# The decay of a running sum, read from PSUM instead of SBUF

## The chip, the cores and the metric

The kernel runs on one core of one Trainium2 chip. The metric is the device time of one execution in microseconds; beside the median of the runs there is one profiled execution, whose rows give every duration used here. The core has a tensor engine (PE, with its weight loads, PEld), a vector engine (DVE), a scalar engine (ACT), GpSimd (POOL) and SyncE (SP), which issues transfers. Each engine takes its instructions in the order in which they stand in its own queue; between engines, semaphores order the work. Data lives in SBUF; PE writes its results to PSUM, from where DVE and ACT read them. POOL and the transfers do not touch PSUM.

## The reference, cut to what matters

Four layers follow one another, each adding to x what it computes from the normalised x: an attention with 49 agents, a two-way running sum (RWKV), a shift with a small convolution, and a long convolution by FFT. x is (32, 192, 56, 56) in float32. Only the second layer is touched:

```python
def step(carry, kv_t):
    p, q, o = carry
    kt, vt = kv_t
    no = jnp.maximum(o, u + kt)
    A = jnp.exp(o - no)
    Bw = jnp.exp(u + kt - no)
    y = (A * p + Bw * vt) / (A * q + Bw)
    ...
    return ((A2 * p + B2 * vt, A2 * q + B2, no2), y)
...
k = jnp.einsum('btc,dc->btd', xs, Wk)
v = jnp.einsum('btc,dc->btd', xs, Wv)
r = jnp.einsum('btc,dc->btd', xs, Wr)
real_w = -jnp.exp(w_decay)
x_fwd = wkv_scan(real_w, u, k, v)
x_bwd = jnp.flip(wkv_scan(real_w, u, jnp.flip(k, 1), jnp.flip(v, 1)), 1)
x_bi = 0.5 * (x_fwd + x_bwd)
h = jax.nn.sigmoid(r) * x_bi
...
out = jnp.einsum('btc,dc->btd', h, Wo)
```

Between the gate and the last product h is normalised over the channels. Without the maxima that keep the exponentials in range, each step is p = d * p + exp(k) * v and q = d * q + exp(k), with one decay d = exp(-exp(w_decay)) for each channel. That is what the kernel's scans compute, over the 3136 pixels of an image, forwards and backwards.

## The kernel before

The layers run one after another on the core: the filter and the attention, then `scan_pairs`, then the channel blocks. A check at the end of `scan_pairs` decides whether a slower guarded form is run in its place; here it isn't.

`scan_pairs` works on images in pairs. The 192 channels of two images make 384 rows, so three tiles of 128: two hold 128 channels of one image each, the third the remaining 64 channels of both. The 3136 pixels are cut into four pieces of 784 (`MC`), so a tile of work is 128x784. There are 16 pairs of images and four pieces, so 64 iterations.

In an iteration, `forwards` for one piece of the next pair and `backwards` for one piece of the present pair run interleaved, with `finish` for the piece before:

- `normed` loads three tiles of x (SP) and normalises them (ACT, L1054).
- `forwards`: PE makes keys and values; ACT takes exp of the keys out of PSUM (L1103), DVE multiplies the values in PSUM by them (L1108). `scan` then makes two running sums for each tile, one over exp(k) v and one over exp(k). ACT inverts the second (L1079, L1080) and DVE multiplies (L1118).
- `backwards`: PE makes the gate r; ACT reads it out of PSUM (L1132) and turns it into a sigmoid (L1136, L1137); `scan` runs in the other direction; then the inverse and three steps on DVE (L1140 to L1142).
- `finish`: PE takes the channel mean away (`centre`), ACT squares out of PSUM (L1157), PE averages the squares (`mean_w`), ACT takes the logarithm out of PSUM (L1166) and the root (L1167); PE multiplies by Wo, DVE scales the product in PSUM (L1180) and adds x (L1183), ACT squares the sum (L1190).

`scan` (L1057 to L1076) issues for each of the two sums: a POOL copy of the carried value into the edge column (L1067), the scan on DVE (L1072), a POOL copy of the last column into the carry (L1073), and one DVE step that adds the present pixel with its bonus (L1074). The scan's operation is out[i] = decay * out[i-1] + data[i]. Its decay is one column of `decay`, a 128x2 tile in SBUF, spread over 784 elements by a stride of zero (column 0 for the first two tiles, column 1 for the third: `of`). An iteration has 12 scans, the stage 768.

PSUM is used up by one pool of four tiles, each 128 x 2 x 512 float32, so two banks of 512. `turned` gives the next of them. A product of 784 pixels fills 392 columns (`HM`) of each bank; columns 392 to 511 of every bank are free. Products for two tiles are written by `_Pairs.outer` (lines 834 and 837), for one tile by `_Pairs.inner` (lines 844 and 847). 17 tiles are taken in an iteration.

The order in the engines' queues is not the order of the text. A scheduler places every instruction, and decides each wait from what the instructions read and write.

Of the kernel before, what the change touches and what calls it, by code (L numbers as in the profile page):

```python
# [7 lines left out]

# [2 lines left out]

# [7 lines left out]
F32 = mybir.dt.float32  # L21
I32 = mybir.dt.int32
AF = mybir.ActivationFunctionType
ALU = mybir.AluOpType
AX = mybir.AxisListType
PSUM = bass.MemoryType.PSUM
# [10 lines left out]
MC = 784  # L37
NM = N // MC
HM = MC // 2
# [26 lines left out]
BANK = 512  # L66
# [784 lines left out]
def scan_pairs(ctx: ExitStack, tc: tile.TileContext, a, k, x1, st_a, st_c, x2, rs2, count):  # L851
# [5 lines left out]
    nc = tc.nc  # L857
# [2 lines left out]
    kp = ctx.enter_context(tc.tile_pool(name="s_k", bufs=3 * NM))  # L860
    wp = ctx.enter_context(tc.tile_pool(name="s_w", bufs=9))
    sp = ctx.enter_context(tc.tile_pool(name="s_s", bufs=2))
    pp = ctx.enter_context(tc.tile_pool(name="s_p", bufs=4, space=PSUM))
    pairs = _Pairs(nc)

    def small(name, shape):
        return cp.tile(shape, F32, name=name, tag=name)

    def turned():
        ps = pp.tile([128, 2, BANK], F32, name="ps", tag="ps")  # L870
        return ps, ps[:, :, :HM], [ps[:, h, :HM] for h in range(2)]

    def parts(t):
# [20 lines left out]
    rows = ((0, 128), (1, 64))  # L894
    cb = small("cb", [128, 2])
    ps, _, _ = turned()
    for out, cols in ((ps[:, 0, 0:1], slice(0, 128)), (ps[0:64, 0, 1:2], slice(128, C)), (ps[64:128, 0, 1:2], slice(128, C))):
        for i, n in rows:
# [20 lines left out]
    decay, near, far = small("decay", [128, 2]), small("near", [128, 2]), small("far", [128, 2])  # L919
# [13 lines left out]
    nc.vector.tensor_tensor(near, near, z, ALU.mult)  # L933
    nc.vector.tensor_tensor(decay, near, far, ALU.add)

    eps = small("eps", [128, 1])
    nc.vector.memset(eps, 4.0 * LN_EPS)
    kept_a, kept_c = small("kept_a", [128, 2, NB // 4, 2]), small("kept_c", [128, 2, NB // 4])
# [5 lines left out]
    def of(t):  # L944
        return slice(0, 1) if t < 2 else slice(1, 2)
# [19 lines left out]
    def grouped(src):  # L965

        n = src[0].shape[1]
        ps, _, _ = turned()
        for t, r in enumerate((slice(0, 64), slice(64, 128))):
            nc.tensor.matmul(ps[:, t, :n], group[0], src[t], start=True, stop=False)  # L970
            nc.tensor.matmul(ps[:, t, :n], group[1][r], src[2][r], start=False, stop=True)
        pairs.inner(group, [ps[:, 1, n : 2 * n]], [[s] for s in src])
        return ps[:, :, :n], ps[:, 1, n : 2 * n]
# [83 lines left out]
    def scan(s, m, t, carry, rev):  # L1057

        b, e = s.bv[m][t], s.ek[m][t]
        c = eu[:, of(t)]  # L1060
        got = []
        for i, src in enumerate((b, e)):
            z = wp.tile([128, MC + 1], F32, name="pq"[i], tag="pq", bufs=5)
            edge, last = (MC, 0) if rev else (0, MC)
            out, before = (z[:, 0:MC], z[:, 1:]) if rev else (z[:, 1:], z[:, 0:MC])
            at = carry[t][i]
            nc.gpsimd.tensor_copy(z[:, edge : edge + 1], at)  # L1067
            if rev:
                out, data = out[:, ::-1], src[:, ::-1]
            else:  # L1070
                data = src[:, :]
            nc.vector.tensor_tensor_scan(out, decay[:, of(t)].to_broadcast([128, MC]), data, at, ALU.mult, ALU.add)  # L1072
            nc.gpsimd.tensor_copy(at, z[:, last : last + 1])  # L1073
            nc.vector.scalar_tensor_tensor(before, src, c, before, ALU.mult, ALU.add)  # L1074
            got.append(before)
        return got  # L1076
# [12 lines left out]
    def forwards(s, m, behind=()):  # L1089
        s.ek[m] = [kp.tile([128, MC], F32, name="ek", tag="ek", bufs=3 * NM + 1) for _ in range(3)]  # L1090
        s.bv[m] = [kp.tile([128, MC], F32, name="bv", tag="bv") for _ in range(3)]
        s.y[m] = [kp.tile([128, MC], F32, name="y", tag="y", bufs=3 * NM + 4) for _ in range(3)]
        xn = normed(s, m)
        for tiles in ((0, 1), (2,)):
            for wt in (wk, wv):
                ps = [turned() for _ in tiles]
                if len(tiles) == 2:
                    pairs.outer(wt, [q[2] for q in ps], xn)
                else:
                    pairs.inner(wt, ps[0][2], xn)  # L1100
                for t, (_, both, _) in zip(tiles, ps):
                    if wt is wk:
                        nc.scalar.activation(  # L1103
                            s.ek[m][t].rearrange("p (h n) -> p h n", h=2), both, AF.Exp,
                            accum_out=s.seen[:, 0, 3 * m + t : 3 * m + t + 1],
                        )
                    else:
                        nc.vector.tensor_tensor(  # L1108
                            s.bv[m][t].rearrange("p (h n) -> p h n", h=2), both,
                            s.ek[m][t].rearrange("p (h n) -> p h n", h=2), ALU.mult,  # L1110
                        )
                if wt is wk and tiles == (0, 1):
                    for later in behind:
                        later()
            for t in tiles:
                num, den = scan(s, m, t, s.fore, False)
                inverse(s, den, m, t, 1)
                nc.vector.tensor_tensor(s.y[m][t], num, den, ALU.mult)  # L1118

    def backwards(s, m):  # L1120

        xn = normed(s, m)
        h = s.y[m]
        for tiles in ((0, 1), (2,)):
            ps = [turned() for _ in tiles]
            if len(tiles) == 2:
                pairs.outer(wr, [q[2] for q in ps], xn)
            else:
                pairs.inner(wr, ps[0][2], xn)
            for t, (_, both, _) in zip(tiles, ps):  # L1130
                g = wp.tile([128, MC], F32, name="g", tag="t")
                nc.scalar.activation(  # L1132
                    g.rearrange("p (h n) -> p h n", h=2), both, AF.Exp, scale=-1.0,
                    accum_out=s.seen[:, 3, 3 * m + t : 3 * m + t + 1],
                )
                nc.scalar.activation(g, g, AF.Ln, bias=1.0)  # L1136
                nc.scalar.activation(g, g, AF.Exp, scale=-1.0)  # L1137
                num, den = scan(s, m, t, s.back, True)
                inverse(s, den, m, t, 2)
                nc.vector.tensor_tensor(num, num, den, ALU.mult)  # L1140
                nc.vector.tensor_tensor(h[t], h[t], num, ALU.add)
                nc.vector.tensor_tensor(h[t], h[t], g, ALU.mult)  # L1142
            yield
# [121 lines left out]
    ps, _, _ = turned()  # L1265
# [502 lines left out]
@with_exitstack  # L1768
def all_blocks(ctx: ExitStack, tc: tile.TileContext, a, k, out):
    nc = tc.nc  # L1770
    NB = out.shape[0]
    dp = ctx.enter_context(tc.tile_pool(name="dram", bufs=1, space=DRAM))

    def scratch(name, shape):
        return dp.tile(shape, F32, name=name, tag=name)

    x1, x2 = scratch("x1", [NB, C, N]), scratch("x2", [C, 2, S + 1, NB // 2, S])
    filt, rs2 = scratch("filt", [C, KS * KS]), scratch("rs2", [C, 2, NB // 4, 2])
    spectra = scratch("spectra", [84, C, 2, 42])
    st_a, st_c = scratch("st_a", [128, 2, NB // 2, 9]), scratch("st_c", [2, 64, 2, NB // 2, 9])  # L1780
    with tc.tile_pool(name="a_r", bufs=1) as rp, tc.tile_pool(name="a_x", bufs=2) as xp:
        ready = _Ready(rp, xp)
        make_filter(tc, a, k, filt, spectra, lambda: ready.load(nc, a, k))
        attention(tc, a, ready, x1, st_a, st_c)
    with tc.tile_pool(name="count", bufs=1) as cp:
        count = cp.tile([1, 1], I32, name="count", tag="count")
        scan_pairs(tc, a, k, x1, st_a, st_c, x2, rs2, count)
        n = nc.values_load(count[0:1, 0:1], min_val=0, max_val=128)
        with tc.If(n > 0):
            scan_guarded(tc, a, k, x1, x2, rs2)  # L1790
    channel_blocks(tc, a, k, x2, rs2, spectra, out)
# [104 lines left out]
```

## Time and profile before

| What | Value |
|---|---|
| Median of 3 runs | 12294.04 us (12291.52 to 12297.86) |
| The profiled execution, its own time | 12294.66 us |
| Its span, first to last instruction | 12292.8 us |
| Granted clock of PE, mean over the span | 0.966 |
| First scan starts; last scan starts | 4919.3 us; 8307.4 us |
| Stage of the scans, 4919 to 8309 | 3390 us |
| Transfers over the span | 59 GB/s |

The span is the time from the first instruction to the last in the profiled execution; its rows add up to this span and not to the median, which comes from other executions. The stage of the scans is about 28% of the span (3390 of 12292.8). A row of the profile names the line, the engine, the operation, the tiles written and read, and their shape; "busy" is the sum of the durations, and durations of neighbouring instructions on one engine overlap a little, so that the time from start to start is shorter than the duration. "Idle before" is time in which the engine had nothing to run, with the instruction that ended it.

### The profile page before, as it was taken

How to read it: one execution, taken by the hardware profiler on the slowest of the kernel's cores; microseconds unless marked ns; L12 is line 12 of the kernel's file. 1: busy time of each engine (PE TensorE's matmuls, PEld its weight loads, DVE VectorE, ACT ScalarE, POOL GpSimd, SP SyncE). 2: the span in 40 equal slices, each digit the busy share in tenths (PEclk: the TensorE clock that was granted, in tenths of full speed). 3: DMA queues.
4: the chain of work that ended last, by engine and by line, in shares of the span. 5: the costliest groups of instructions: out<-in, count | busy, mean ns of one | idle time of the engine just before them, and what ended most of it. 6: DMA issues, size and time to landing. Idle time of an engine off the chain costs nothing. (4 is left out here: it accounts for less than half of the span.)

```text
span 12292.8 us, 164375 instructions
## 1 busy us (share of the span) xinstructions
PE 11329.2 (92%) x62734; PEld 7107.7 (58%) x62734; DVE 10836.4 (88%) x15489; ACT 6205.0 (50%) x11808; POOL 2250.7 (18%) x2228
## 2 busy tenths in 40 slices
PE   7999999999999999788888888888999999999999
PEld 3555555655555555333333333336777777777777
DVE  6888888888888887999999999997888888888888
ACT  3555555555555554566666666663333333333333
POOL 0000000000000000655555555551000000000000
PEclk9999999999999999999999999999999999999999
DMA  2111111111111111244344433442111111111111
GB/s 69 40 42 46 52 41 40 40 40 40 40 40 40 42 50 44 75 103 100 95 97 103 101 94 97 103 101 65 44 41 45 41 44 42 44 42 44 42 43 29
DMA packets 930055, 719.69 MB, mean 59 GB/s; under 512 B 770325, under 2 KB 807236, under 8 KB 920124
## 3 DMA queue, kind: packets, MB, share of 16 engines
q1 hardware_dynamic: 919020, 683.39, 21.7%
q10 hardware_dynamic: 10240, 25.70, 0.8%
q8 instruction: 500, 8.19, 0.3%
q14 instruction: 295, 2.42, 0.1%
HBM read 403.47 MB, written 240.65 MB: 52 GB/s over the span
## 5 line engine op out<-in xcount | busy, mean ns | idle before, releaser
L572 DVE SCALAR_TENSOR_TENSOR o<-v_a,att_w,o 128x896 f32<-128x896 f32 (+1 forms) x1024 | 1053.8, 1029 | 418.6 <-ACT v_a L546 291.5
L1763 ACT COPY y<-ps 64x252 f32<-64x252 f32 (+1 forms) x2376 | 808.2, 340 | 1135.0 <-PE ps L1757 1104.8
L1681 PE MATMUL ps<-fixed,real 84*84 84x112 f32 x6144 | 1090.9, 259 | 0.0
L1681 PE MATMUL ps<-fixed,imag 84*84 84x112 f32 x6144 | 1089.5, 259 | 0.0
L1688 ACT COPY z<-ps 84x448 f32<-84x448 f32 x768 | 405.6, 528 | 1218.5 <-PE ps L1681 1217.0
L1086 POOL MEMSET f<- 128x1 f32 x96 | 8.9, 99 | 4726.3 <-DMA st_c<-st 4721.3
L1681 PEld LDWEIGHTS ps<-fixed,real 84*84 84x84 f32 x6144 | 784.0, 153 | 134.2 <-issue 95.8
L1681 PEld LDWEIGHTS ps<-fixed,imag 84*84 84x84 f32 x6144 | 763.8, 153 | 0.0
L1079 ACT ACTIVATE q<-q 128x784 f32<-128x784 f32 x384 | 328.2, 855 | 802.5 <-DVE q L1074 633.1
L834 PE MATMUL ps<-sq,fixed 128*128 128x392 f32 x512 | 297.3, 743 | 428.6 <-ACT sq L1157 428.6
L572 DVE SCALAR_TENSOR_TENSOR o<-v_c,att_w,o 128x448 f32<-128x448 f32 (+1 forms) x1024 | 635.0, 620 | 5.1
L585 PE MATMUL ps<-xs_a,gk_a 128*98 128x448 f32 (+1 forms) x1536 | 637.1, 495 | 0.0
L589 ACT ACTIVATE pr<-ps,low 98x896 f32<-98x896 f32 (+1 forms) x384 | 352.3, 918 | 559.9 <-DVE low L587 559.9
L586 PE MATMUL ps<-xs_c,gk_c 125*98 125x448 f32 (+1 forms) x1536 | 631.6, 492 | 0.0
L1547 POOL TENSOR_TENSOR mat<-tap,tap 114x114 f32<-114x114 f32 x96 | 40.8, 425 | 3166.1 <-PE ps L1607 2313.2
L677 PE MATMUL ps<-gq_a,xs_a 128*112 128x294 f32 x1792 | 602.8, 417 | 19.2 <-DVE pq L682 19.2
L1698 PE MATMUL ps<-z,fixed 84*114 84x448 f32 x1536 | 608.8, 539 | 0.0
L834 PE MATMUL ps<-x,weights 128*128 128x392 f32 x1536 | 577.4, 519 | 27.5 <-DVE bv L1108 14.2
L678 PE MATMUL ps<-gq_c,xs_c 125*112 125x294 f32 x1792 | 594.5, 412 | 0.0
L1655 PE MATMUL re<-y,fixed 128*84 128x420 f32 (+1 forms) x1152 | 532.3, 543 | 8.7 <-ACT y L1763 7.6
L1655 PE MATMUL im<-y,fixed 128*84 128x420 f32 (+1 forms) x1152 | 526.9, 538 | 0.0
L690 ACT ACTIVATE pq<-pq 112x1176 f32<-112x1176 f32 x224 | 265.3, 1184 | 498.9 <-DVE pq L682 376.0
(367 smaller groups left out, 29245.2 us busy)
## 6 DMA issues: line engine op xcount, KB each, us to landing
x<-x SPq DMA_DIRECT2D x576, 392.0 KB
x<-x SPq DMA_DIRECT2D x512, 196.0 KB
x<-x SPq DMA_DIRECT2D x192, 399.0 KB
out_x<-x SPq DMA_DIRECT2D x384, 196.0 KB
x<-in_x SPq DMA_DIRECT2D x32, 1568.0 KB
x<-x SPq DMA_DIRECT2D x32, 1568.0 KB
x<-in_x SPq DMA_DIRECT2D x64, 392.0 KB
rd<-rd ACTq DMA_DIRECT2D x128, 196.0 KB
```

The source lines that it names most:

```text
L572: nc.vector.scalar_tensor_tensor(dst, tap(i), dww[:, t, i : i + 1], dst, ALU.mult, ALU.add)
L585: mm(ps[P2, h, :n], g[:, cols], xs_a[j][:, px], start=True, stop=False)
L586: mm(ps[P2, h, :n], gk_c[0:KC, 2 * j + h, cols], xs_c[j][0:KC, px], start=False, stop=True)
L589: nc.scalar.activation(pr[:, :, :n], ps[P2, :, :n], AF.Exp, bias=low[:, j, p : p + 1], accum_out=sums[:, j, p : p + 1])
L677: mm(ps[:SUB, i, :HA], xs_a[j][:, px], g, start=True, stop=False)
L678: mm(ps[:SUB, i, :HA], xs_c[j][0:KC, px], gq_c[0:KC, 2 * j + (q + i) // ns], start=False, stop=True)
L834: mm(out, aa, srcs[t][h], start=True, stop=False)
L1655: nc.tensor.matmul(ps[:, : n * 84], f2[:, i, :], y[:, i0 : i0 + n].rearrange("p g s u -> p (g s u)"), start=True, stop=True)
L1681: nc.tensor.matmul(ps[:84, i * 2 * S : (i + 1) * 2 * S], part[:, i0 + i].rearrange("p s u -> p (s u)"), f3[:, m, :], start=(m == 0), stop= ...
L1688: nc.scalar.copy(z[:, i0 : i0 + n].rearrange("p g m w -> p (g m w)"), ps[:84, : n * 2 * S])
L1698: nc.tensor.matmul(got, f4[:, m, :], z[:, i0 : i0 + n, m, :], start=(m == 0), stop=(m == 1))
L1763: nc.scalar.copy(y[64 * m : 64 * m + 64, 2 * g0 + i : 2 * (g0 + n) : 2], got[64 * i : 64 * i + 64, :, :, m, :])
```

## The change

The pool of four tiles becomes four tiles that are made once, each with a name of its own (`ps0` to `ps3`), and `turned` gives them in turn. As they live for the whole stage, something may be kept in them: the two columns of `decay` are copied into columns 392 and 393 of the first bank of the first tile, where no product is written, and the scans read this copy, `pace`, in place of `decay`.

```diff
+import itertools
...
-    pp = ctx.enter_context(tc.tile_pool(name="s_p", bufs=4, space=PSUM))
+    pp = ctx.enter_context(tc.tile_pool(name="s_p", bufs=1, space=PSUM))
     pairs = _Pairs(nc)
+
+    banks = [pp.tile([128, 2, BANK], F32, name=f"ps{i}", tag=f"ps{i}") for i in range(4)]
+    turns = itertools.cycle(banks)
...
     def turned():
-        ps = pp.tile([128, 2, BANK], F32, name="ps", tag="ps")
+        ps = next(turns)
         return ps, ps[:, :, :HM], [ps[:, h, :HM] for h in range(2)]
...
     nc.vector.tensor_tensor(decay, near, far, ALU.add)
 
+
+    pace = banks[0][:, 0, HM : HM + 2]
+    nc.vector.tensor_copy(pace, decay)
     eps = small("eps", [128, 1])
...
-            nc.vector.tensor_tensor_scan(out, decay[:, of(t)].to_broadcast([128, MC]), data, at, ALU.mult, ALU.add)
+            nc.vector.tensor_tensor_scan(out, pace[:, of(t)].to_broadcast([128, MC]), data, at, ALU.mult, ALU.add)
```

Nothing else is edited. The scheduler orders the stage anew with the changed accesses.

## The prediction

> **What bounds the kernel now.** I began with the page's busy times: no engine is full over the whole span, so the stage of the scans has to be read alone. The scans' own line gives its bounds: the first of 768 starts at 4919 us, the last at 8307.4, so the table by windows was asked for 4919 to 8309.
>
> ```profile
> PE 11329.2 (92%) x62734; PEld 7107.7 (58%) x62734; DVE 10836.4 (88%) x15489; ACT 6205.0 (50%) x11808; POOL 2250.7 (18%) x2228
> ```
>
> ```profile
> 4919.00:8309.00 3390.00, 2808.14 (x10237) 1277.79 (x10236) 3296.25 (x3377) 2148.40 (x3691) 1922.99 (x1698) 0.92 0.39 97
> ```
>
> In the stage the columns are PE, PEld, DVE, ACT, POOL. DVE works 3296 of 3390 us (97%) and is idle 94; PE is busy 2808 (83%). Nothing can be gained except by shorter DVE instructions or out of those 94 us. Next the groups of instructions of DVE and POOL in the same window (busy, mean ns, idle before them):
>
> ```profile
> L1072 DVE TENSOR_TENSOR_SCAN p<-decay,b,bv 128x784 f32<-128x784 f32 x192 | 353.6, 1842 | 0.0
> L1074 DVE SCALAR_TENSOR_TENSOR p<-bv,eu,p 128x784 f32<-128x784 f32 x384 | 386.8, 1021 | 0.1
> L1140 DVE TENSOR_TENSOR p<-p,q 128x784 f32<-128x784 f32 x190 | 183.8, 968 | 12.4 <-ACT q L1080 12.1
> L1108 DVE TENSOR_TENSOR bv<-ps,ek 128x784 f32<-128x784 f32 x192 | 180.3, 965 | 4.9 <-PE ps L837 4.9
> L1180 DVE TENSOR_TENSOR sq<-ps,rd 128x784 f32<-128x784 f32 x186 | 178.6, 968 | 60.7 <-PE ps L837 55.7 <-ACT q L1079 1.9 <-ACT g L1136 1.7
> L1073 POOL COPY f<-p 128x1 f32<-128x1 f32 x192 | 338.9, 1765 | 316.9 <-DVE p L1072 309.0
> ```
>
> A scan costs 1.84 us where any other 784-element operation costs 0.96 to 1.02. The idle time is mostly 61 us before the products with Wo (L1180), which wait for PE; a scan waits for ACT only where its keys come late (19 us, 9 of them at the start). POOL copies one column in 1.77 us, yet DVE waits for none of them. Last PE's line of time, around one iteration:
>
> ```profile
> 6500.79 5.60 PE L834 MATMUL ps<-sq,fixed 128*128 128x392 f32 x8 [8.83 <-ACT sq L1157]
> 6506.32 1.89 PE L837 MATMUL ps<-sq,fixed 64*128 64x392 f32 x8
> ...
> 6518.45 2.90 PE L834 MATMUL ps<-x,weights 128*128 128x392 f32 x8
> 6521.28 1.59 PE L837 MATMUL ps<-x,weights 64*128 64x392 f32 x8
> ...
> 6527.15 1.58 PE L844 MATMUL ps<-x,weights 128*128 128x392 f32 x4
> 6528.66 1.54 PE L847 MATMUL ps<-x,weights 128*64 128x392 f32 x8
> ```
>
> A group for two tiles takes 4.35 us (6518.45 to 6522.80), for one tile 2.98 (6527.15 to 6530.13, where the next begins); two records are one matmul. After 8.83 us of waiting the same eight first records take 5.53 us in place of 2.83: PE comes back at a lower clock.
>
> **Part 1: the scan's operand.** 768 scans read their decay from PSUM. No row has a scan with a PSUM operand. From below: the nearest one-pass row, L1074 at 1.02, would give 768 x (1.84 - 1.02) = 630 us back. From above: L1108 and L1180 read PSUM, L1140 reads only SBUF, and they differ by at most 3 ns; even 10 ns would be 8 us. I take zero: L1140 and L1074 have two SBUF operands of four bytes and run one element per step, so that pair is not what makes the scan take two. The trace's scan takes one step more per element than L1074 (0.82 us over 784 elements). [...]
>
> **Part 2: POOL.** The copies before and behind each scan (L1067, L1073) may get shorter, since a scan now has one SBUF operand. DVE waits for no copy, so nothing is gained; ACT's wait for POOL at L1079 is hidden, because DVE waits for ACT's inverses (L1140) only 12 us in the stage. That 12 us is the most this can bring.
>
> **Part 3: the bank.** This is where I see the cost. `pace` lies in columns 392 and 393 of the first bank of tile 0, and a matmul group that writes tile 0 begins in this bank. The instruction order of the changed program with its waits shows the ordering by bank, not by column: 193 matmul groups into tile 0 wait for a scan, and scans wait behind ACT's readers of tile 0 (39 times L1132, 33 L1166, 22 L1157) and 18 times for PE. Before there was neither. 280 uses of tile 0 lie in 193 windows between two scans. In a window DVE may do only what isn't a scan, while PE fills tile 0 and ACT or DVE empties it. Both queues are in order: behind the matmul that waits stand the groups of the other three tiles, and behind the scan that waits stands all of DVE. And as the order bunches four to eight scans (1.76 us apart), PE waits up to ten microseconds and returns slow.
>
> Cost of a window = length of the hand-over less DVE's other work in it. DVE's work by start-to-start times in its line of time: 0.95 for L1074, 0.88 for a two-operand step. The kinds, with their counts in the order:
> - Centre, square, mean, Ln (25 windows): half a two-tile group at the slow clock (half of 5.53, plus 1.52 for its half-row matmuls with no partner beside them) 4.3; ACT's second inverse pass, which stands in front, 0.85; square 0.8; mean group 4.35; two Ln of 0.8: 11.9. DVE has two L1074 and six steps, 7.2. Missing 4.7: 118 us. In 8 more the gate's group follows on tile 0 in place of the Ln: 11.9 - 1.6 + 2.98 + 0.8 = 14.1, missing 6.9: 55 us.
> - Wo after the scans, then the next pair's keys and values (22): rest of the Wo pair 3.0 (half of 2.90, plus 1.59), its third tile 2.98, keys 4.35, values 4.35: 14.7 before the first product L1108, against 9.2 of DVE work: 5.5 each, 121 us.
> - The same with Wo already under way (29): in 22 PE begins 1.2 late, finishing the group of the window before, and has the Wo pair, its third tile, keys and values (16.0) to do against two scans and 10.1 of other work (13.6), 3.6; in 7 only today's 1.3 (55.7 us over the 42 waits of L1180 for PE): 88 us.
> - Third tile's keys (8): slow one-tile group 2.98 x 5.53/2.83 = 5.8, ACT 0.8, against two L1074 and a step, 2.78: 3.8, 30 us.
> - One group and one reader (43): between 0 and (half-group and half-rows 3.0 + 0.8 - 1.83) 2.0; nearer to the upper end, as DVE's step in the window waits for ACT's two inverse passes too: 1.5, 65 us.
> - The other 58: 5.4 to 6.3 us of DVE work over one group and one reader (at most 4.35 + 0.8): nothing. If that cover goes, 58 x 2 = 116 us.
>
> Sum 477 us. It takes the place of today's waits for PE and ACT before the same steps (L1180 61, L1140 12, L1072 19 less the 9 at the start: 83): +394. Bounds: if every hand-over were hidden, minus 94 (all idle time gone); if nothing ran beside any of the 280 uses, 280 x (4.35 + 0.8) = 1442. I keep the sum between them, since the rows decide it window by window.
>
> **Part 4: the rest.** The four tiles were in turn before as well (a pool of four), so the turn itself moves nothing. One copy of 128x2 in the set-up, about 0.15 us by rows of such size. SP's loads of x get their issue later when PE is late; today ACT waits about 8 us for them in the inner stage and the DMA share is 0.39, so I add nothing. The attention and the channel blocks keep their order, instruction for instruction.
>
> So the span becomes 12292.8 + 394 = 12686.8, with the 1.9 us around it (12294.66 less 12292.8) 12688.7; on the median 12294.04, which lies 0.6 below that execution, 12688.
>
> **Rivals.**
> - The scan runs in one pass (faster). Place: L1072; price 1.02 us. 630 us come off DVE, leaving 2666, and hand-overs of 477 stay at least: 3143, or 247 below 3390: 12047. PE's 2808 us then presses too, so up to 12200. It decides from a scan below 1.84 - 394/768 = 1.33 us. For it: one of its two SBUF streams goes away. Against it: L1074 and L1140. 7%.
> - The hand-overs are hidden. Warm clock and halves written early give 2.2 + 0.8 + 4.35 + 0.9 = 8.3 against 7.2 in the first kind: 33 x 1.1 = 36; 51 x 1.3 = 66 for Wo; the rest none. 102 - 83 = +19: 12313, and up to 12420 if only part is. For it: DVE has 1947 us of work that isn't a scan against 280 uses. Against it: PE has only 582 us to spare. 13%.
> - PE stays at the slow clock (1.95 times) through the second and third kinds (Wo) too: one two-tile group more at half speed is 4.1 us, in 51 windows 209: 12897 and beyond. For it: waits of ten microseconds. Against it: 4 records later, in L837 after the slow eight, the rate is back. 8%.
>
> **Numbers.** My forecast, 12688, has 72%. The range is 12400 to 12950: it leaves out the one-pass scan (7%), most of the hidden hand-overs (8%) and the far side of the slow clock (5%). Faster by over 0.2%: the one-pass scan and a little of the hidden case, 0.08. Within 0.2% (25 us, what a measurement of this kernel can tell from no change; the three runs spread over 6): 0.05. Slower: 0.87.
>
> **What would show it.** Scan rows at 1.82 to 1.86 us. DVE's busy time unchanged near 3296 in a stage of some 3780 us, with idle time before L1072 put down to ACT L1166 and L1132, and before L1108 and L1180 put down to PE. PE waiting for DVE L1072 for hundreds of microseconds (today 7 in all) and a mean granted clock in the stage below today's 0.92. POOL copies shorter. Wrong if: scan rows near 1.0; L1072 with no wait for ACT; or DVE idle still near 94.

## The result, and the profile after

The changed kernel takes 12913.75 us (median of 4 runs, 12909.12 to 12919.05) against 12293.69 for the kernel before on the same chip: a ratio of 1.0504, 95% interval 1.0486 to 1.0522. The forecast was 12688 with a range of 12400 to 12950. Sign and mechanism are as forecast; the loss is 620 us where 394 were forecast, and one term of the sum makes up nearly half of the difference.

The page's busy times and its row of granted clock, then the table by windows for the stage of the scans (its length, then busy time of PE, PEld, DVE, ACT, POOL, the granted clock, the DMA share and GB/s):

```profile
PE 11748.3 (91%) x62734; PEld 7232.2 (56%) x62734; DVE 10875.9 (84%) x15490; ACT 6242.6 (48%) x11808; POOL 1359.7 (11%) x2228
...
PEclk9999999999999998888888888888999999999999
```

```profile
4937.00:8947.00 4010.00, 3228.24 (x10275) 1406.39 (x10275) 3337.03 (x3381) 2194.34 (x3704) 1032.93 (x1698) 0.87 0.33 83
```

The stage alone is longer: 4010 us from its first scan to the end of its last, 3390 before. DVE's work in it is nearly the same: by the trace's rows 3337 us after and 3297 before, overlaps counted once. So of the 620 us, 580 are idle time of DVE (93 before, 673 after). The other 40 fit the ends of instructions, which an instruction right behind would have overlapped: durations exceed start-to-start times by some 80 ns (a scan takes 1.84 us, and the next instruction starts 1.76 behind its start). PE lost as well: 420 us more busy for the same matmuls, at a clock of 0.87 in place of 0.92.

The groups of DVE and POOL in the stage (busy, mean ns of one, idle before them and what ended it):

```profile
L1079 DVE TENSOR_TENSOR_SCAN p<-ps,b,bv 128x784 f32<-128x784 f32 x192 | 354.4, 1846 | 292.2 <-ACT rd L1173 175.6 <-ACT g L1139 112.7 <-PE ps L838 3.5
L1115 DVE TENSOR_TENSOR bv<-ps,ek 128x784 f32<-128x784 f32 x192 | 181.1, 970 | 210.4 <-PE ps L838 148.8 <-ACT ek L1110 30.8 <-PE ps L848 30.8
L1187 DVE TENSOR_TENSOR sq<-ps,rd 128x784 f32<-128x784 f32 x186 | 178.5, 970 | 65.5 <-PE ps L838 65.5
```

```profile
L1080 POOL COPY f<-p 128x1 f32<-128x1 f32 x192 | 58.3, 303 | 992.0 <-DVE p L1079 992.0
```

The same scan reads `ps` in place of `decay` and takes 1846 ns against 1842: for the scan's decay PSUM is as good a source here as SBUF. POOL's copy behind it went from 1765 ns to 303, and nothing came of it. What is new is the idle time: 292 us before the first backward scan of a pair, which waits for ACT's readers of tile 0 (L1173 the logarithm, L1139 the gate), and 210 before the product of the values (L1115), which waits for PE. PE in turn waits for scans; its largest waits in the stage (us in total, times, longest):

```profile
PE ps L835 <- DVE q L1079: 347.4, 74, 10.6
PE ps L835 <- ACT sq L1164: 151.9, 70, 5.7
PE ps L845 <- DVE q L1079: 149.9, 54, 5.8
```

Before, all waits of PE for scans came to 7 us (of its weight loads: 6.1 and 1.2). One dear window, in the line of time (start, duration; in brackets the wait before it):

```profile
6608.85 1.83 DVE L1079 TENSOR_TENSOR_SCAN q<-ps,b,ek 128x784 f32<-128x784 f32 x1
...
6610.73 2.98 PE L835 MATMUL ps<-y,fixed 128*128 128x392 f32 x4 [9.94 <-DVE q L1079]
...
6613.64 2.98 PE L838 MATMUL ps<-y,fixed 64*128 64x392 f32 x4
...
6617.62 5.28 PE L835 MATMUL ps<-sq,fixed 128*128 128x392 f32 x8 [1.00 <-ACT sq L1164]
...
6622.83 1.59 PE L838 MATMUL ps<-sq,fixed 64*128 64x392 f32 x8
6624.35 1.58 PE L845 MATMUL ps<-x,weights 128*128 128x392 f32 x4
6624.45 1.72 ACT L1173 ACTIVATE rd<-ps,eps 128x784 f32<-128x784 f32 x2 [5.27 <-PE ps L838]
...
6626.20 1.85 DVE L1079 TENSOR_TENSOR_SCAN p<-ps,b,bv 128x784 f32<-128x784 f32 x1 [6.98 <-ACT rd L1173]
```

Between two scans (6608.85 and 6626.20) tile 0 changes hands twice over: centre group, square, group of means, logarithm. PE has waited 9.94 us for the scans, comes back at half its rate (the granted clock is 0.50 from 6605.40 to 6622.46), and is slow in the half centre group (5.9 us) and in the group of means too (6.7 us, 6617.62 to 6624.35). DVE has 7.6 us of other work, stands for 1.0 within it (for ACT's inverse) and then for 6.98.

### The profile page after: what moved, and what is told of

It reads as the page before. It is cut to its first block, busy times and chain, and to the rows that moved or that the text cites. A ratio compares the mean times of both kernels' runs of the same rounds, so it can differ in the third digit from the quotient of the medians.

```text
span 12917.2 us, 164427 instructions
## 1 busy us (share of the span) xinstructions
PE 11748.3 (91%) x62734; PEld 7232.2 (56%) x62734; DVE 10875.9 (84%) x15490; ACT 6242.6 (48%) x11808; POOL 1359.7 (11%) x2228
## 5 line engine op out<-in xcount | busy, mean ns | idle before, releaser
L835 PE MATMUL ps<-y,fixed 128*128 128x392 f32 x512 | 278.0, 677 | 407.6 <-DVE q L1079 308.1
L1079 DVE TENSOR_TENSOR_SCAN p<-ps,b,bv 128x784 f32<-128x784 f32 x192 | 354.4, 1846 | 292.2 <-ACT rd L1173 175.6
```

What stands on the lines that cost most here:

```text
L835: mm(out, aa, srcs[t][h], start=True, stop=False)
```

## The experiments

Below, "order" is the order in which the instructions of a version stand in the engines' queues, "stage" the time from the first scan to the end of the last in its profile, "idle" DVE's idle time in it, and "waits" the matmul groups that wait for a scan in the order. The kernel before has 3390, 93 and none; the changed kernel 4010, 673 and 193. Edits are against the changed kernel unless said otherwise. e4 to e7 were executed twice each, the others four times or more.

| Version | Waits | Median us | Ratio to before, 95% | Stage | Idle |
|---|---|---|---|---|---|
| e1 turn only | 0 | 12289.51 | 0.9984 to 1.0003 | 3381 | 85 |
| e2 tile 0 for the decay alone | 0 | 12398.2 | 1.0070 to 1.0103 | 3463 | 172 |
| e2b three tiles, decay in SBUF | 0 | 12368.57 | 1.0040 to 1.0074 | 3463 | 163 |
| e3 forward scans only | 96 | 12452.47 | 1.0108 to 1.0142 | 3542 | 240 |
| e4 backward scans only | 127 | 12536.97 | 1.0164 to 1.0224 | 3645 | 327 |
| e5 tile 0 once in seven | 159 | 12577.53 | 1.0197 to 1.0257 | 3665 | 348 |
| e6 two copies, in tiles 0 and 2 | 385 | 12652.76 | 1.0258 to 1.0318 | 3747 | 414 |
| e7 copy in the second bank of tile 0 | 193 | 12913.78 | 1.0470 to 1.0531 | 4009 | 671 |
| e8 centre and means never in tile 0 | 221 | 12596.76 | 1.0225 to 1.0259 | 3688 | 363 |
| e10 only centre and means in tile 0 | 64 | 12992.27 | 1.0544 to 1.0580 | 4089 | 753 |
| e11 one scan of each pair | 193 | 12613.16 | 1.0237 to 1.0271 | 3713 | 398 |
| e12 as e10, PE kept warm | 64 | 12765.85 | 1.0370 to 1.0405 | 3867 | 535 |

### Is it the turn, the operand, or the bank? (e1, e2, e2b)

e1 keeps the four named tiles and gives the scans `decay` in SBUF again:

```diff
-    pace = banks[0][:, 0, HM : HM + 2]
-    nc.vector.tensor_copy(pace, decay)
...
-            nc.vector.tensor_tensor_scan(out, pace[:, of(t)]...
+            nc.vector.tensor_tensor_scan(out, decay[:, of(t)]...
```

> Only the four tiles taken in turn; the scans read their decay from SBUF. Theory A (the bank: the loss is the ordering between the scans and whoever writes or reads the first bank of tile 0): no scan is ordered against that bank any more, so 12294, within 15 us; DVE idle in the stage near 93 us. Rival B (the loss lies in the fixed tiles and the new order, wherever the decay is): near 12914.

12289.51 us, no different from before. The turn itself costs nothing.

e2 leaves tile 0 to the decay alone; the products take turns in the other three (`turns = itertools.cycle(banks[1:])`). e2b does the same and has the scans read SBUF, as in e1.

> The decay stays in PSUM, in tile 0, but the products take turns in the other three tiles alone, so no product shares the decay's bank. Theory A: the scans cost what they cost from SBUF; the time is that of three tiles with the decay in SBUF, within 15 us, well below 12914 (12294 to 12450, according to what the fourth tile was worth). [...]

> Three tiles in turn, the decay in SBUF: the reference for the own bank. Theory A: equal to it within 15 us. It also prices the fourth tile: 0 to 150 us above 12294, as DVE's present waits for PE (61 us) can grow by the third less room. [...]

The stages are 3463.0 and 3463.1 us. So in the profiled executions the operand in PSUM costs nothing in the stage, with three tiles in both. The medians lie 30 us apart, which is twice the 15 at most of the theory. The two profiled executions are only 5 us apart (12376.16 and 12371.61); the other three of e2 took 12397 to 12417, at a granted clock of 0.965 to 0.967 where the profiled one had 0.972. No trace shows in which stage they took longer. The scan's rows by form, for the version with the decay alone in tile 0:

```profile
L1079 DVE TENSOR_TENSOR_SCAN p<-ps,f,bv 128x784 f32<-128x784 f32 x192 | 354.5, 1846 | 1.2
L1079 DVE TENSOR_TENSOR_SCAN q<-ps,f,ek 128x784 f32<-128x784 f32 x192 | 350.9, 1827 | 0.0
```

and for the one with the decay in SBUF:

```profile
L1077 DVE TENSOR_TENSOR_SCAN q<-decay,f,ek 128x784 f32<-128x784 f32 x192 | 348.4, 1841 | 75.7 <-ACT ek L1108 75.6
L1077 DVE TENSOR_TENSOR_SCAN p<-decay,f,bv 128x784 f32<-128x784 f32 x192 | 346.6, 1833 | 0.0
```

No form of either is apart from the other by more than 15 ns, and the sign differs between p and q. With nobody else in the decay's tile no scan waits for a reader of it, and POOL's copies are about as short as in the changed kernel (from 5000 to 8300 us POOL's mean instruction takes 0.67 us, there 0.60, in the kernel before 1.14): their relief is worth nothing. Taking a tile away costs 73 us of stage against the kernel before (3463 less 3390), 82 against e1.

### Which scans, and how many uses of tile 0? (e3, e4, e5, e7)

e3 and e4 read `(decay if rev else pace)` and `(pace if rev else decay)`; e5 takes tile 0 once in seven turns (`itertools.cycle(banks + banks[1:])`); e7 puts the copy into the other bank of tile 0 (`banks[0][:, 1, HM : HM + 2]`).

> Only the 384 forward scans read PSUM; the backward scans read SBUF. Theory A, from the windows of the changed kernel's trace: the kinds that end on a backward scan (277 us of idle time) and those that begin with PE held by one (Wo: 234) fall back to today's (81), the windows among forward scans stay (30 + 27 + 17 and some more): 12294 + 90, so 12340 to 12460. Rival B (loss spread over all scans alike): half of 620, so 12600.

> The mirror of the forward-only kernel: only the 384 backward scans read PSUM. Theory A, by the windows of the changed kernel's trace: the kinds that end on a backward scan (277 us idle) and those where PE was held by one before Wo (131 + 103 + 15) stay, less today's 81: 12294 + 440, so 12640 to 12820. Rival B (loss spread over all scans alike): the same as forward-only, 12450.

> As the changed kernel, but tile 0 is taken once in seven turns (0, 1, 2, 3, 1, 2, 3) in place of once in four: 160 uses in place of 280, and 159 matmul groups wait for a scan in place of 193. Theory A: the loss goes with the hand-overs, 620 x 159/193 = 510 at most and 620 x 160/280 = 354 at least: 12640 to 12810. Rival B (order and fixed tiles): unchanged near 12914.

> The copy lies in the second bank of tile 0. Its waits count as many as in the changed kernel (193, 94 and 18). Theory A: the same hand-overs, since a group writes both banks before its reader takes both; a group's first matmuls may now go ahead of the wait, so 12860 to 12920. Rival (the first bank matters, as PE is stopped before it has written anything): gain of 100 us or more.

e3 is where it was expected. e4 and e5 are below their ranges by 103 and 62 us. Both ranges came from the kinds of windows and the uses of tile 0 in the changed kernel; but every version gets an order of its own, in which the windows are of other kinds too. In e5 only 3 of the 159 waits are centre groups, where the changed kernel has 33 of 193, and the scans' wait for the logarithm fell from 175.6 us to 1.6. In e4 the order has all 33, and that wait is 67.5; why it is so much less was not taken apart. e7 is the changed kernel again, 12913.78. The order is even wider than by bank: all 193 waits stand at the first matmul of a group, which writes the first bank, though the copy now lies in the second. The trace has it so too:

```profile
6600.47 2.98 PE L835 MATMUL ps<-y,fixed 128*128 128x392 f32 x4 [9.95 <-DVE q L1079]
```

So the tile is handed over as a whole, and it makes no difference which of its banks holds the copy.

### The count of waits is not the price (e6)

e6 gives p and q a copy each, in tiles 0 and 2 (`paces[i]`).

> The cost doubled: one copy of the decay in tile 0 for the scans of p, one in tile 2 for the scans of q. 385 matmul groups wait for a scan in place of 193. Theory A: slower than 12914 by a third of the loss or more, 13120 or above, as every second group now meets a scan. Rival: if one held bank is enough to bring PE to a stop, a second adds little: 12914 to 13000.

A clear miss. PE waits for scans twice as often (385 against 193), yet the loss is smaller than with one copy: 354 us in place of 620. PE's largest waits in its stage:

```profile
PE ps L835 <- DVE p L1080: 290.4, 61, 7.1
PE ps L845 <- DVE p L1080: 72.0, 33, 6.2
```

They are shorter (at most 7.1 us; 10.6 in the changed kernel), and the windows between scans cost less. Most waits of the order are also over before PE comes to them: PE stands for a scan 142 times in e6 (443 us) and 128 times in the changed kernel (497 us). My theory of one price per wait fell here. Two things could be behind it: in e6 a scan of the other kind may run while one tile is handed over, and PE rests less before it is needed. The next four runs take these apart.

### What a free scan is worth (e11)

p reads SBUF, q reads tile 0: `(decay, pace)[i][:, of(t)]`. The number of waits is that of the changed kernel.

> Edit: the first scan of each pair (p) reads its decay from SBUF, the second (q) from tile 0; the four tiles in turn. The order has as many waits of PE for scans as the changed kernel (193), but DVE may run one scan of 1.85 us in a window. Theory (a window costs the hand-over less DVE's other work in it): 1.85 us less in each of the 33 + 51 + 8 windows of the dear kinds and about half of that in 43 more: 170 + 40 = 210 less, 12914 - 210 = 12700, 12650 to 12760; it would also be what made the version with two tiles cheaper than the changed kernel. Rival (the count of waits decides): 12880 to 12930.

12613 us, 37 below the range: 301 less than the changed kernel at the same 193 waits. The wait moved from p to q:

```profile
L1079 DVE TENSOR_TENSOR_SCAN p<-decay,b,bv 128x784 f32<-128x784 f32 x192 | 353.4, 1841 | 0.0
L1079 DVE TENSOR_TENSOR_SCAN q<-ps,b,ek 128x784 f32<-128x784 f32 x192 | 352.3, 1835 | 95.7 <-ACT rd L1173 52.0 <-ACT g L1139 43.1 <-PE ps L838 0.3
```

96 us before the backward q in place of 292 before the backward p. A scan of 1.84 us that may run in the window takes time off it. By its own length 210 us less were expected; the other 91 of the 301 fit an order that changes with it, and were not taken apart. That this is also what makes e6 cheap fits, but was not shown for e6 by itself.

### Where the dear windows are (e8, e10)

`turned` gets a set of tiles and gives the least recently used of them. In e8 the groups for centre and means may take tiles 1 to 3 and all others any; in e10 it is the other way round.

```diff
-    def turned():
-        ps = next(turns)
+    def turned(allowed=(0, 1, 2, 3)):
+        i = next(i for i in queue if i in allowed)
+        queue.remove(i)
+        queue.append(i)
+        ps = banks[i]
...
-            ps = [turned() for _ in tiles]
+            ps = [turned((1, 2, 3)) for _ in tiles]
...
-        pv = [turned() for _ in range(2)]
+        pv = [turned((1, 2, 3)) for _ in range(2)]
```

> Edit: the groups of `finish` that make the centre and the mean of squares take tiles 1 to 3 only; every other group takes the least recently used of the four. Tile 0 is used by 192 groups in place of 272, and PE waits for a scan 221 times in the order in place of 193. Theory (the slow clock in the centre and mean windows made up 277 of the 620 us): those windows disappear, 12294 + 620 - 277 = 12637, and up to 74 more because the other groups press on three tiles: 12610 to 12720. Rival (each wait of PE for a scan costs the same): 620 x 221/193 = 710, so 12930 to 13080.

> Edit: only the groups for centre and mean may take tile 0 (128 uses, 64 waits of PE for a scan, one for each half image, at the same place in the iteration); all others take tiles 1 to 3. Theory (this kind costs 8.6 us each, PE coming back slow after the scans): 64 x 8.6 = 550, and 74 for the three tiles of the others: 12780 to 12960, with DVE's scans waiting for ACT about 450 us or more and PE groups of 5 us and more behind the waits. Rival (each wait costs the same 620/193 = 3.2 us): 64 x 3.2 = 205, and 74: 12540 to 12600. Second rival (the order hides windows that come this rarely, twelve scans apart): the 74 alone, 12370 to 12420.

This is the clearest pair. With 221 waits, none of them in the centre and mean groups, 12597 (13 below the theory's range and 330 or more below the rival's). With 64 waits, all of them there, 12992: the dearest version of all, 32 above the theory's range, where a price per wait gives 12540 to 12600. In e10, DVE's largest waits:

```profile
DVE p L1081 <- ACT rd L1175: 378.6, 62, 7.5
DVE bv L1117 <- PE ps L837: 197.8, 61, 11.6
DVE p L1149 <- ACT q L1089: 140.1, 121, 2.0
```

379 us over 62 windows is 6.1 us for each wait for the logarithm; the 198 us over 61 products of values come one step on, as PE makes the keys and values behind the late groups. The three kinds of wait together make 716 us, 11.6 for each of 62 iterations.

### Is it the clock? (e12)

e12 is e10 with twelve matmuls of constants in each iteration, whose result nothing reads:

```diff
+        spare = turned((1, 2, 3))[2][0]
+        for _ in range(12):
+            nc.tensor.matmul(spare, weights[:, 0:128], weights[:, 128 : 128 + HM], start=True, stop=True)
         sqs = [parts(t) for t in sq]
```

> Edit on the version in which only centre and mean take tile 0: 12 more matmuls of constants (weights by weights, 128x392, into a tile that nothing reads) per iteration. In the order 9 of them stand on PE ahead of the centre group that waits for the scans and 2 to 3 between it and the group of means; DVE's order stays nearly the same. Computes nothing that is used. Theory (the windows are dear because PE comes back slow): at the rate of 0.38 us per record the half of the centre group takes 3.0 in place of 5.9 us and the group of means 4.35 in place of 6.6; less up to 1.6 us for the matmuls in between, 3.5 to 5.2 us less in each of 61 windows: 12992 - 215 to 320, so 12670 to 12780, with DVE's waits for ACT's `rd` near 100 us in place of 379. Rival (the length of the chain with its waits, not the clock, sets the window): 12970 to 13100.

More work for PE, and 226 us less: 12765.85 against 12992.27, inside the range, near its upper end. By the ratios to the kernel before, 1.0388 against 1.0562, it is 214. The waits of DVE answer as expected for the first kind, and not for the others:

```profile
DVE p L1149 <- ACT q L1089: 187.6, 120, 4.9
DVE bv L1117 <- PE ps L837: 177.1, 59, 4.2
DVE p L1081 <- ACT rd L1178: 102.9, 63, 13.9
```

The wait for the logarithm went from 379 us to 103. PE's groups for centre and means, e10 first and then e12 (count, busy, mean ns of a record, idle before them):

```profile
L834 PE MATMUL ps<-y,fixed 128*128 128x392 f32 x504 | 332.9, 808 | 622.5 <-DVE q L1081 436.7 <-DVE bv L1117 132.7 <-DVE rs L1001 26.6
...
L834 PE MATMUL ps<-sq,fixed 128*128 128x392 f32 x496 | 284.4, 740 | 65.7 <-ACT sq L1166 65.7
```

```profile
L834 PE MATMUL ps<-y,fixed 128*128 128x392 f32 x504 | 243.2, 614 | 218.6 <-DVE bv L1117 130.8 <-DVE q L1081 76.8 <-DVE rs L1001 5.4
L834 PE MATMUL ps<-sq,fixed 128*128 128x392 f32 x504 | 177.3, 495 | 1.0 <-ACT sq L1166 1.0
```

A record of the group of means takes 495 ns in place of 740, one of the centre group 614 in place of 808; the granted clock of the stage is 0.95 in place of 0.86. One window in e12's line of time:

```profile
6501.40 2.43 PE L834 MATMUL ps<-y,fixed 128*128 128x392 f32 x4 [4.14 <-DVE bv L1117]
6503.75 2.98 PE L837 MATMUL ps<-y,fixed 64*128 64x392 f32 x4
6506.66 2.98 PE L844 MATMUL ps<-y,fixed 128*128 128x392 f32 x4
6509.57 2.84 PE L847 MATMUL ps<-y,fixed 128*64 128x392 f32 x8
6512.34 6.85 PE L1172 MATMUL ps<-weights 128*128 128x392 f32 x20
6519.03 1.48 PE L834 MATMUL ps<-y,fixed 128*128 128x392 f32 x4
6520.44 1.58 PE L837 MATMUL ps<-y,fixed 64*128 64x392 f32 x4
```

The wait ahead of the last centre half is filled (L1172), and the half takes 3.0 us, where the window shown of the changed kernel had 5.9. The slow spell is still there, but it falls on the halves that DVE doesn't wait for. At 343 of the 3179 places of the stage DVE's queue holds another instruction than in e10, but all scans except 4 of 768 stand where they stood. So a small part of the gain may come from the new order; the shorter records and the wait for the logarithm, 276 us less by itself, are in the rows. This shows the clock as a cause of this kind's price; it doesn't make the version good. No version is faster than the kernel before: e1 alone equals it, and it differs from it only in how the four tiles are made.

## Why the prediction was right in sign and low in size

**Part 1, the operand: right.** Taken as nothing. The rows stayed at 1.83 to 1.85 us, and e2 and e2b have equal stages in their profiled executions (3463.0 and 3463.1 us). The time of one step for an element is in the rows of the kernel before: the same kind of operation as L1074 takes 677 ns for 448 elements and 1146 for 896, so 1.05 ns each:

```profile
L572 DVE SCALAR_TENSOR_TENSOR o<-v_a,att_w,o 128x448 f32<-128x448 f32 x256 | 173.4, 677 | 0.0
L572 DVE SCALAR_TENSOR_TENSOR o<-v_a,att_w,o 128x896 f32<-128x896 f32 x768 | 880.4, 1146 | 418.6 <-ACT v_a L546 291.5 <-ACT o L570 124.9
```

The 0.82 us by which the scan is longer than L1074 are 1.05 ns for each of 784 elements as well, and they stayed with the decay in PSUM. Why the scan takes that second step, no run shows; the one-pass rival (12047) is out.

**Part 2, POOL: right.** Copies shorter (1765 to 303 ns for one form, POOL's busy time in the stage 1923 to 1033 us), no gain. That the operand in SBUF is what lengthens them fits e3 and e4: from 5000 to 8300 us POOL's mean instruction takes 1.14 us where all scans read their decay in SBUF (the kernel before), 0.92 and 0.82 where half of them do, and 0.60 where none does (the changed kernel).

**Part 3, the bank: right in its mechanism, its first term mis-sized.** Idle time by kind of window, counted in the trace after by the operations of DVE between two scans, so that the numbers of windows differ a little from those by the order:

| Kind of window | Forecast us | Measured us |
|---|---|---|
| Centre, square, mean, Ln (33) | 118 + 55 = 173 | 277 (33 windows) |
| Wo after the scans, then keys and values (22) | 121 | 131 (22) |
| The same with Wo under way (29) | 88 | 103 (29) |
| Third tile's keys (8) | 30 | 30 (8) |
| One group, one reader (43), and the other 58 | 65 + 0 | 132 |

The step that failed is "half a two-tile group at the slow clock ... 4.3 ... mean group 4.35", in the first kind. I took the clock as slow for the first half of the centre group alone. In the window shown the half group took 5.9 us (1.6 more) and the group of means 6.7 (2.4 more): 4.0 us more. Over all 33 windows the trace has 8.4 us each (277 over 33) where I had 5.2, so the step is 104 us short. That this kind is dear, and that the clock is a cause, e8, e10 and e12 show. Rows of the kernel before spoke against the step already. The line that I read as PE's return, slow for 5.5 us (6500.79), is a group of means, which took 7.3 us there, and the stage's rows have this group slow on average:

```profile
L834 PE MATMUL ps<-sq,fixed 128*128 128x392 f32 x496 | 291.5, 751 | 428.6 <-ACT sq L1157 428.6
L834 PE MATMUL ps<-y,fixed 128*128 128x392 f32 x502 | 191.5, 514 | 65.8 <-DVE bv L1108 64.2 <-DVE sq L1180 1.6
```

A record of the means took 751 ns before the change and 777 after; there it cost nothing, as DVE did not wait for it. The centre group's records were warm (514 ns) and became slow (680). I priced the means by the group of keys (4.35 us), not by their own row. The rest: 67 us in the last row of the table, where I put nothing for the 58; 25 in the two kinds with Wo; and 40 of DVE's ends uncovered, which the sum didn't have. So 104 + 67 + 25 + 40 = 236, less 10 because I set 83 us of today's idle time against the sum where all 93 went into it: 226, which is 620 less 394.

Ahead of the stage, the first scan starts 18 us later (4937.4 against 4919.3), and about 14 come back behind it: the span grew by 624, the stage by 620. Of the 18 about 12.6 are there already when the set-up's first products are made, and 9.4 of them at 359 us, inside the attention, whose order is unchanged; in e1, e2, e2b, e7 and e10 that place lies 0.7 us earlier to 7.9 later than in the kernel before. So most of the 18 isn't shown to come from the change.

**Part 4, the rest: nearly right.** The turn moves nothing (e1). The loads I left at nothing: ACT's wait for them before it normalises x went from 17.5 us to 138.5 in the stage, while SP waits for PE to release their buffers (2325 us for L845; 1927 for the same matmuls before). It is not among the largest waits of DVE; a price of its own was not measured.

**The rivals.** The hidden hand-overs (12313) are out. "PE stays at the slow clock" gave 12897, 17 below the measured time, but not for its reason: it put the slow clock into the Wo windows, and those came out as forecast (131 and 103). The slow clock lay in the first kind.

**What would show it.** Scan rows, DVE's busy time, the waits of L1079 for L1173 and L1139, and a clock below 0.92 (0.87) came as written; the stage is 4010, not 3780.

## What to carry to other kernels

Here a value that is kept in a PSUM tile which is also in turn for matmuls had all its readers ordered against all writers and readers of that tile (193 waits in the order, none before), and even the two banks of a tile were ordered as one (e7). The reading itself was free (1846 ns against 1842), and a tile of its own avoided the waits (e2), at the price of a buffer (73 us of stage). The price of such a hand-over is not counted in waits (620 us for 193, 354 for 385 in e6): read it from the line of time, as the chain from one scan to the next less the work that may run in between, with PE at the rate at which it really comes back. Where PE waits long and then stands on the critical path, look at the duration of its records first (740 ns for one of the means in e10, 495 in e12).

## What the hardware showed that I had not expected

PE's slow spell has no fixed length here. By the granted clock in the traces, PE worked at half rate for 6.2 us after a wait of 8.83 in the kernel before (6500.79 to 6506.97), and for 11.7 us with a pause of 1.0 after 9.94 in the changed kernel (6610.73 to 6622.46). In e12, after 4.14, the clock fell 0.6 us behind PE's return and stayed at half for 10.2 us of work without a pause (6502.00 to 6512.24). In the first two windows it had fallen before PE's return, 4.8 and 4.6 us into the wait (6496.73 and 6605.40). Every half-rate spell in the stages of these three lasts a whole number of 3.41 us: one, two or three in e12 (18, 7 and 25 of 50), the same in the kernel before (13, 22 and 29 of 65) but for a single spell of six, and up to six in the changed kernel (44, 31, 15, 1, 14 and 14 of 119). What decides the number of steps is open.

The order that is seen here, for two columns that no product writes, goes by the whole tile of two banks (e7: 193 waits at the first matmul of a group, with the copy in the other bank). That the hardware needs it, no run shows, as none took the order away.
